# x loaded first, LayerNorm statistics ahead of the low matrices, and a prologue with one PSUM bank per block

## The chip, the cores and the metric

The kernel runs on one core of a Trainium2 chip. The metric is the device time of one execution in microseconds (us), the median of several. The engines are TensorE (PE in the profile, PEld its weight loads), VectorE (DVE), ScalarE (ACT), GpSimd (POOL) and SyncE (SP), which issues most of the transfers.

## The reference

A "macaron" block on x of 8 sequences, 512 tokens, 256 channels, all in float32:

```python
x = x + 0.5 * ffn(layernorm(x))
x = x + attn(layernorm(x))      # 16 heads, causal softmax, queries/keys/values of 2 x 256
x = x + 0.5 * ffn(layernorm(x)) # the same weights again

def ffn(x):
    h = x @ W_exp + b_exp                       # 256 -> 1024
    h = butterfly(h, up_weights, 1024)          # 10 stages of 2x2 mixing, stride 1, 2, ..., 512
    h = gelu(h + up_bias)                       # exact gelu
    h = butterfly(h, down_weights, 1024)        # 10 more stages
    return h @ W_con + b_con + down_bias        # 1024 -> 256
```

A butterfly is linear. The reference applies it to the activations.

## The kernel before

The kernel folds the butterflies into the weights first, in a prologue, and then works on the eight sequences with two plain matrices, `wup_sb` (256 to 1024) and `wdn_sb` (1024 to 256). The 1024 hidden features are 8 blocks (`NBLK`) of 128.

**The prologue.** The seven stages of small stride stay inside a block, so for each block they are one 128 x 128 matrix. `low_matrices` builds all eight on VectorE out of a table (`upe_sb`): six multiplications that double the width each time, from 32 to 1024 elements per partition (L225). `low_up` multiplies each with its rows of `wexp_sb` on PE (L254), 257 columns, the last one the bias. A float32 matmul is two passes in the profile. The three stages of large stride pair whole blocks. `high_stage` does one: per block ScalarE writes a product with the block's own coefficient (`mine`, L238), and VectorE adds the partner block times the other coefficient (L243). The result lies in `high_up`. `finish_up` transposes it on PE (`pup`, L269), four transposes to a PSUM bank, in the order first half of the blocks with both halves of the channels, then second half; ScalarE and VectorE copy the banks to `wup_sb` in turn. For the down side the same is done from `dne_sb` and `wcon_sb`, with `low_down` at the end (L275).

In between stands the first LayerNorm, of sequence 0: `ln_stats` (VectorE: two `bn_stats` and two `bn_aggr` per half and one addition, ten instructions in all; POOL: one power, `rstd`, per half), `ln_apply` on POOL (`xn`, L174, four instructions) and, in `ln_steps`, eight transposes on PE into two banks (`pxt`, L197), which ScalarE copies to `xnt` (L198). The first dense matmuls of the kernel, `ph_f` (L309), need both `xnt` and `wup_sb`. `keep_busy(19)` has PE multiply the identity with itself until `low_up` can run (`idle`, L261).

The order is written out by hand (`manual_schedule`): each engine executes its instructions in the order of the program text, here

```python
        keep_busy(19)
        mats = low_matrices(upe_sb, "up")
        cur = low_up(mats)
        run([partial(ln_stats, 0, "f1", half) for half in range(2)])
        run([partial(ln_apply, 0, "f1", half, nc.gpsimd) for half in range(2)])
        for i in range(HIGH):
            cur, whole = high_stage(cur, i, upc_sb, "up", C + 1, NBLK)
        run(ln_steps(0, "f1", copy=nc.scalar.copy))
        finish_up(cur, whole)
```

and waits are on semaphores between engines, per tile: two engines' accesses to one PSUM tile are put in order, reads too.

**PSUM.** It has eight banks. The kernel before has three pools from start to end: `ps_u` (one tile of four banks), `ps_o` (one bank) and `ps_a` (three single banks). `low_up` uses all of them: its first four blocks share the one tile of `ps_u`, the next three take the banks of `ps_a`, the last takes `ps_o`, which `idle` used before. `pxt` and `pup` then go round in the three banks of `ps_a`, so that each waits for the copy out of the tile three places earlier: the second `pup` bank takes the one that ScalarE's first copy to `xnt` has read.

**Transfers.** SP's queue issues, in this order: the two parts of `upe_sb` (0.5 MB each), the first half of `wexp_sb`, x of sequence 0, the second half of `wexp_sb`, then `dne_sb`, `wcon_sb` and the rest. ScalarE's queue brings the coefficients `upc_sb`.

**After the prologue** a table `ORDER` sets, for each sequence, how the steps of attention of one sequence and of the two feed-forward parts of its neighbours follow on one another.

Of the kernel before, what the change touches and what calls it, by code (L numbers as in the profile page):

```python
# [36 lines left out]
F32 = mybir.dt.float32  # L37
BF16 = mybir.dt.bfloat16
AF = mybir.ActivationFunctionType
# [3 lines left out]
P = 128  # L43
# [5 lines left out]
def macaron_kernel(  # L49
# [18 lines left out]
    nc = tc.nc  # L68
    B, N, C = x.shape
# [13 lines left out]
    lnp = ctx.enter_context(tc.tile_pool(name="ln", bufs=2))  # L83
    work = ctx.enter_context(tc.tile_pool(name="work", bufs=1))
    dram = ctx.enter_context(tc.tile_pool(name="dram", bufs=2, space=bass.MemoryType.DRAM))
    ps_u = ctx.enter_context(tc.tile_pool(name="ps_u", bufs=1, space=bass.MemoryType.PSUM))
    ps_o = ctx.enter_context(tc.tile_pool(name="ps_o", bufs=1, space=bass.MemoryType.PSUM))
    ps_a = ctx.enter_context(tc.tile_pool(name="ps_a", bufs=3, space=bass.MemoryType.PSUM))


    fold = ctx.enter_context(ExitStack())
    fold_pool = fold.enter_context(tc.tile_pool(name="fold", bufs=1))
    upc_sb = fold_pool.tile([P, HIGH, NBLK, 2], F32, name="upc_sb")
    dnc_sb = fold_pool.tile([P, HIGH, NBLK, 2], F32, name="dnc_sb")
    upb_sb = const.tile([P, NBLK], F32, name="upb_sb")
# [9 lines left out]
    def load_x(b):  # L105
        xt[b] = resid.tile([P, NT, C], F32, name=f"x_{b}", tag="x", bufs=4)
        nc.sync.dma_start(out=xt[b], in_=x[b].rearrange("(t p) c -> p t c", p=P))
# [10 lines left out]
    wexp_blocks = wexp_t.rearrange("(n p) c -> p n c", p=P)  # L118
    first, second = slice(0, NBLK // 2), slice(NBLK // 2, NBLK)
    with tc.manual_schedule():  # L120
        nc.sync.dma_start(out=upe_sb[:, :last], in_=up_e[:, :last])
        nc.sync.dma_start(out=upe_sb[:, last:], in_=up_e[:, last:])
        nc.sync.dma_start(out=wexp_sb[:, first, :], in_=wexp_blocks[:, first, :])
        load_x(0)
        nc.sync.dma_start(out=wexp_sb[:, second, :], in_=wexp_blocks[:, second, :])
        nc.scalar.dma_start(out=upc_sb, in_=up_c)
        nc.sync.dma_start(out=dne_sb, in_=dn_e)
        nc.sync.dma_start(out=wcon_sb, in_=wcon.rearrange("(n p) c -> p n c", p=P))
        nc.sync.dma_start(out=dnc_sb, in_=dn_c)
        nc.sync.dma_start(out=upb_sb, in_=up_b)  # L130
        nc.sync.dma_start(out=bc_sb, in_=b_con.to_broadcast([P, C]))
        nc.sync.dma_start(out=db_sb, in_=dn_b.to_broadcast([P, C]))
        load_x(1)
        for w_sb, w in ((wq_sb, wq), (wk_sb, wk), (wv_sb, wv), (wo_sb, wo)):
            nc.sync.dma_start(out=w_sb, in_=w.rearrange("(k p) f -> p k f", p=P))
        for b in range(2, 4):
            load_x(b)


    ident = const.tile([P, P], F32, name="ident")  # L140
    make_identity(nc, ident)

# [60 lines left out]
    def low_matrices(tables, net):  # L203

        at, mat = 0, None
        for step in range(LOW):  # L210
            half = 1 << step
            mine = tables[:, at : at + NBLK * 2 * half].rearrange("p (n e) -> p n e", n=NBLK)
            at += NBLK * 2 * half
            if mat is None:
                mat = mine
                continue
            new = fold_pool.tile([P, NBLK, 2 * half], F32, name=f"mat_{net}_{step}", tag=f"mat_{step % 2}")
            if net == "up":
                dims, old = "p n (a r) -> p n a r", mat.rearrange("p n (o r) -> p n o r", o=1)
                shape = dict(a=2)  # L220
            else:
                dims, old = "p n (m b) -> p n m b", mat.rearrange("p n (m o) -> p n m o", o=1)
                shape = dict(b=2)
            view = new.rearrange(dims, **shape)
            nc.vector.tensor_tensor(view, mine.rearrange(dims, **shape), old.to_broadcast(view.shape), ALU.mult)  # L225
            mat = new
        return mat

    def high_stage(cur, i, coef, net, width, on_scalar):

        tag = "wexp" if net == "dn" and i == 1 else f"high_{net}_{i % 2}"
        new = fold_pool.tile([P, NBLK, C + 1], F32, name=f"high_{net}_{i}", tag=tag)[:, :, :width]
        mine = []
        for blk in range(NBLK):
            mine.append(fold_pool.tile([P, width], F32, name=f"mine_{net}_{i}_{blk}", tag="mine", bufs=NBLK))
            w_self = coef[:, i, blk, 0:1]
            if blk < on_scalar:
                nc.scalar.activation(mine[blk], cur[blk], AF.Copy, scale=w_self)  # L238
            else:
                nc.gpsimd.tensor_scalar(mine[blk], cur[blk], w_self, 1.0, ALU.mult, ALU.mult)  # L240
        for blk in range(NBLK):
            w_other = coef[:, i, blk, 1:2]
            nc.vector.scalar_tensor_tensor(new[:, blk, :], cur[blk ^ (1 << i)], w_other, mine[blk], ALU.mult, ALU.add)  # L243
        return [new[:, blk, :] for blk in range(NBLK)], new

    def low_up(mats):

        four = ps_u.tile([P, 4, 512], F32, name="low_up", tag="u")
        banks = [four[:, i, :] for i in range(4)]
        banks += [ps_a.tile([P, 512], F32, name=f"low_up_{i}", tag="a") for i in range(3)]  # L250
        banks.append(ps_o.tile([P, 512], F32, name="low_up_o", tag="pa"))
        got = [bank[:, : C + 1] for bank in banks]
        for blk in range(NBLK):
            nc.tensor.matmul(got[blk], lhsT=mats[:, blk, :], rhs=wexp_sb[:, blk, :], start=True, stop=True)  # L254
        return got

    def keep_busy(times):

        idle = ps_o.tile([P, 512], F32, name="idle", tag="pa")
        for _ in range(times):  # L260
            nc.tensor.matmul(idle[:, :P], lhsT=ident, rhs=ident, start=True, stop=True)  # L261

# [16 lines left out]
    def ln_steps(b, what, **how):  # L279
        def new():  # L280
            kept["xnt", what, b] = work.tile([P, 4, KC, P], F32, name=f"xnt_{what}_{b}", tag="xnt", bufs=2)
            return kept["xnt", what, b]

        def step(kc):
            transposed(b, what, kept["xnt", what, b] if kc else new(), kc, **how)

        def write():
            td = kept["td", what, b] = dram.tile([P, 4, KC * P], F32, name=f"td_{what}_{b}", tag="td")
            nc.sync.dma_start(out=td, in_=kept.pop(("tx", what, b)).rearrange("p j k t r -> p j (k t r)"))

        def read():

            xnt = new().rearrange("p i k n -> p i (k n)")
            td = kept.pop(("td", what, b)).rearrange("(i s) j e -> j s i e", i=4)
            for j in range(4):
                nc.sync.dma_start(out=xnt[bass.ts(j, 32)], in_=td[j])

        if by_dma(b, what):
            return [write, read]
        return [partial(step, kc) for kc in range(KC)]  # L300
# [217 lines left out]
    def lns(b, what):  # L518

        return [partial(f, b, what, half) for f in (ln_stats, ln_apply) for half in range(2)]  # L520

    def run(*steps):
        for step in steps:
            if isinstance(step, list):
                run(*step)
            else:
                step()
# [99 lines left out]


    with fold, tc.manual_schedule():
        keep_busy(19)  # L630
        mats = low_matrices(upe_sb, "up")
        cur = low_up(mats)
        run([partial(ln_stats, 0, "f1", half) for half in range(2)])
        run([partial(ln_apply, 0, "f1", half, nc.gpsimd) for half in range(2)])
        for i in range(HIGH):
            cur, whole = high_stage(cur, i, upc_sb, "up", C + 1, NBLK)
        run(ln_steps(0, "f1", copy=nc.scalar.copy))
        finish_up(cur, whole)
        up = up_steps(0, "f1")
        mats = low_matrices(dne_sb, "dn")  # L640
        cur = [wcon_sb[:, blk, :] for blk in range(NBLK)]
        for i in range(HIGH - 1, -1, -1):
            cur, _ = high_stage(cur, i, dnc_sb, "dn", C, NBLK if i == HIGH - 1 else NBLK // 2)
            run([up.pop(0) for _ in range(min(3, len(up)))])
        nc.vector.tensor_tensor(bhalf, bc_sb, db_sb, ALU.add)
        nc.vector.tensor_scalar(bhalf, bhalf, 0.5, None, ALU.mult)
        low_down(mats, cur)
        run(partial(ffn_bias, 0, 0), partial(ffn_bias, 0, 1))
        run(lns(1, "f1"))

    with tc.tile_pool(name="attn", bufs=1) as attn, tc.manual_schedule():
        for b in range(B):
            sequence(b, attn)
# [77 lines left out]
```

## Time and profile before

| What | us |
|---|---|
| median of 3 runs | 886.3 |
| lowest and highest run | 885.77, 886.96 |
| the profiled execution | 884.92 |
| its span, first to last instruction | 883.1 |
| PE busy | 862.1 (98%) |
| VectorE busy | 628.0 (71%) |
| ScalarE busy | 520.1 (59%) |
| POOL busy | 87.1 (10%) |

Times in the profile count from the start of the span. The page cuts the span in 40 slices of 22 us and gives the busy share of each engine in tenths, and the clock that PE was granted, in tenths of full speed. The chain of waits is followed back from the last instruction to what released it, step by step. In rows of the timeline the first number is the start, the second the time that the row covers, "x8" the number of instructions in it, and the brackets say how long the engine was idle before, and what ended that. A row of a window that ends early can cover fewer instructions than the one of the whole stretch.

### The profile page before, as it was taken

What the parts mean: (1) busy time and instruction counts of PE and PEld (TensorE: products, weight loads), DVE (VectorE), ACT (ScalarE), POOL (GpSimd) and SP (SyncE); (2) the same over time, 40 slices, a digit from 0 to 9 for tenths busy, and PEclk for the clock granted to TensorE, in tenths of its full rate; (3) what the DMA queues carried; (4) which work ended last, traced back from release to release, by engine and by line L of the source; (5) the groups of instructions that cost most, each with busy time, mean ns of one, the idle gap of its engine ahead of it and who ended that gap; (6) DMA issues with size and microseconds to landing.
All of it is one profiled execution on the core that took longest, in us unless ns stands there. A gap on an engine that the chain in (4) does not pass through costs nothing.

```text
span 883.1 us, 13289 instructions
## 1 busy us (share of the span) xinstructions
PE 862.1 (98%) x4334; PEld 499.9 (57%) x4334; DVE 628.0 (71%) x1814; ACT 520.1 (59%) x1360; POOL 87.1 (10%) x103
## 2 busy tenths in 40 slices
PE   7999999999999999999999999999999999989988
PEld 5564644655546555555645646557555463745656
DVE  7957894998567775887758876877577775978230
ACT  5718676655495565875467663874458664746211
POOL 3420000021002010011102001021000000010010
PEclk8999999999999999999999999999999999999999
DMA  9210766548665667165774367666665477377600
GB/s 325 70 48 2 194 190 159 146 111 227 155 156 154 155 160 200 45 183 156 200 180 102 91 169 194 176 162 160 170 165 126 123 186 191 97 183 193 154 13 24
DMA packets 52964, 130.16 MB, mean 147 GB/s; under 512 B 10912, under 2 KB 32672, under 8 KB 52896
## 3 DMA queue, kind: packets, MB, share of 16 engines
q1 hardware_dynamic: 52752, 129.30, 55.5%
q8 instruction: 34, 0.56, 0.3%
q14 instruction: 34, 0.28, 0.1%
q10 hardware_dynamic: 144, 0.02, 0.0%
HBM read 21.80 MB, written 15.20 MB: 42 GB/s over the span
## 4 chain that ended last, share of the span: by engine, by line
PE 84%; DVE 8%; ACT 3%; DMA 2%; SPq 1%; issue 1%; POOL 0%; DVEq 0%; ACTq 0%; POOLq 0%
PE py_f L329 23%; PE ph_f L309 23%; PE pp L354 12%; PE sc L408 9%; PE pa L488 6%; PE pv L372 5%; PE po L509 5%; DVE e L422 4%; ACT e L435 2%; SPq L475 1%; DVE pr L453 1%; DVE high_up L243 1%; PE idle L261 1%; DMA td_f<-tx_f 1%; PE pup L269 0%
## 5 line engine op out<-in xcount | busy, mean ns | idle before, releaser
L435 ACT ACTIVATE e<-e,nm 128x128 f32<-128x128 f32 (+3 forms) x512 | 280.3, 549 | 112.7 <-DVE nm L422 112.4
L422 DVE CUSTOM_DVE_ANT_0 e<-sc,mask 128x128 f32<-128x128 f32 (+3 forms) x512 | 216.3, 485 | 117.2 <-PE sc L408 117.0
L329 PE MATMUL py_f<-wdn_sb,g_f 128*128 128x256 f32 x1024 | 232.7, 382 | 0.0
L309 PE MATMUL ph_f<-xnt_f,wup_sb 128*128 128x512 f32 x512 | 229.3, 596 | 1.1 <-ACT v L375 0.7
L329 PEld LDWEIGHTS py_f<-wdn_sb,g_f 128*128 128x128 f32 x1024 | 192.2, 190 | 43.8 <-issue 17.1
L453 DVE STREAM_TRANSPOSE pr<-e 128x1536 f32<-128x1536 f32 (+2 forms) x128 | 170.6, 1354 | 21.0 <-ACT e L435 20.9
L309 PEld LDWEIGHTS ph_f<-xnt_f,wup_sb 128*128 128x128 f32 x512 | 95.6, 190 | 113.3 <-issue 101.4
L316 ACT ACTIVATE g_f<-ph_f,bup_sb 128x512 f32<-128x512 f32 x128 | 85.2, 686 | 116.4 <-PE ph_f L309 116.0
L408 PE MATMUL sc<-kt,qt 32*128 32x128 f32 (+3 forms) x1024 | 92.2, 461 | 6.1 <-DVE nm L422 4.4
L435 ACT ACTIVATION_READ_ACCUMULATOR e<-e,nm 128x1 f32 x512 | 95.7, 187 | 0.0
L488 PE MATMUL pa<-pt,v 128*32 128x512 f32 (+3 forms) x1024 | 75.6, 435 | 1.8 <-issue 1.0
L408 PEld LDWEIGHTS sc<-kt,qt 32*128 32x128 f32 x1024 | 44.4, 183 | 57.2 <-issue 23.8
L160 POOL TENSOR_TENSOR rstd_f<-mv_f,mhalf 128x2 f32<-128x2 f32 x32 | 22.7, 710 | 483.4 <-DVE mv_f L158 483.3
L488 PEld LDWEIGHTS pa<-pt,v 128*32 128x32 f32 x1024 | 30.6, 109 | 57.8 <-issue 50.8
L354 PE MATMUL pp<-xnt_at,wq_sb 128*128 128x512 f32 x128 | 61.4, 602 | 0.0
L338 DVE SCALAR_TENSOR_TENSOR x<-py_f,x 128x512 f32<-128x512 f32 (+1 forms) x34 | 22.2, 652 | 55.2 <-PE py_f L329 55.2
L354 PE MATMUL pp<-xnt_at,wk_sb 128*128 128x512 f32 x128 | 60.9, 598 | 0.0
L509 PE MATMUL po<-wo_sb,ot 128*128 128x256 f32 x256 | 59.4, 384 | 0.0
L372 PE MATMUL pv<-wv_sb,xnt_at 128*128 128x512 f32 x128 | 59.1, 597 | 0.0
L435 ACT ACT_TABLE_LOAD x29 | 37.2, 1283 | 33.7 <-DVE nm L422 33.6
L509 PEld LDWEIGHTS po<-wo_sb,ot 128*128 128x128 f32 x256 | 47.6, 190 | 12.3 <-issue 4.7
L191 POOL TENSOR_TENSOR x<-x,bhalf 128x512 f32<-128x512 f32 x32 | 40.7, 1273 | 134.2 <-DVE xn_f L174 113.6
(74 smaller groups left out, 547.3 us busy)
## 6 DMA issues: line engine op xcount, KB each, us to landing
pt<-pr SPq DMA_DIRECT2D x512, 176.0 KB, 4.0
td_f<-tx_f SPq DMA_DIRECT2D x14, 512.0 KB, 5.0
xnt_f<-td_f SPq DMA_DIRECT2D x56, 128.0 KB, 3.0
x<-in_x_dram SPq DMA_DIRECT2D x8, 512.0 KB, 6.6
td_at<-tx_at SPq DMA_DIRECT2D x7, 512.0 KB, 2.6
xnt_at<-td_at SPq DMA_DIRECT2D x28, 128.0 KB, 3.1
out_dram<-x SPq DMA_DIRECT2D x14, 256.0 KB, 4.3
wexp_sb<-in_wexp_t_dram SPq DMA_DIRECT2D x2, 514.0 KB, 6.8
```

The source lines that it names most:

```text
L191: nc.gpsimd.tensor_tensor(x2, x2, bhalf.rearrange("p (o c) -> p o c", o=1).to_broadcast([P, 2, C]), ALU.add)
L309: nc.tensor.matmul(ph[:, :N], lhsT=wup_sb[:, kc, bass.ts(fc, P)], rhs=xnt[:, :, kc, :].rearrange("p i (t r) -> p t i r", r=32), start=(kc ...
L316: nc.scalar.activation(g[:, fc, :], ph[:, :N], AF.Gelu, bias=bup_sb[:, fc : fc + 1])
L329: nc.tensor.matmul(py[:, i, :], lhsT=g[:, fc, bass.ts(t, P)], rhs=wdn_sb[:, fc, :], start=(fc == 0), stop=(fc == NBLK - 1),)
L354: nc.tensor.matmul(pp[:, :N], lhsT=w[:, kc, bass.ts(g, P)], rhs=xnt[:, :, kc, :], start=(kc == 0), stop=(kc == KC - 1),)
L372: nc.tensor.matmul(pp, lhsT=xnt[:, t, kc, :], rhs=wv_sb[:, kc, :], start=(kc == 0), stop=(kc == KC - 1))
L408: nc.tensor.matmul(sc[:, j, at : at + n], lhsT=kept["q", b, gg][r, bass.ts(qb, P)], rhs=kept["k", b, gg][r, :n], start=(i == 0), stop=True ...
L422: nc.vector.tensor_tensor_reduce(out=e[:, j, at : at + n], in0=sc[:, j, at : at + n], in1=mask[:, N - n :], scale=-1.0, scalar=3.0e38, op0 ...
L435: nc.scalar.activation(e[:, j, at : at + n], e[:, j, at : at + n], AF.Exp, scale=-1.0, bias=nm[:, qb, gg, j : j + 1], accum_out=zs[:, gg, ...
L453: nc.vector.transpose(pr[:, :, :, qb : qb + 3 * n - 2 : 3, :].rearrange("p j h k r -> p h k j r"), blocks[:, :, :n])
L488: nc.tensor.matmul(by_row[r, :, kb * 32 :], lhsT=v[:, kb, bass.ds(g * P + j * HD, HD)], rhs=pt[:, :, bass.ds(j * NSLOT + SLOT[kb] + kb, NT ...
L509: nc.tensor.matmul(po[:, i, :], lhsT=ot[:, g, bass.ts(t, P)], rhs=wo_sb[:, g, :], start=(g == 0), stop=(g == NG - 1))
```

## The change

- x of sequence 0 is the first transfer on SP's queue; `upe_sb`'s two parts and the first half of `wexp_sb` come behind it. The second half of `wexp_sb` and all later transfers keep their places.
- `ln_stats` and `ln_apply` of sequence 0 stand ahead of `low_matrices`: VectorE does the ten statistics instructions first and then the six multiplications; POOL's `rstd` and `xn` follow the statistics as before.
- A tile `ones` of two elements is set by VectorE, and ScalarE's first instruction is a one-element activation on it, which takes the activation table load with it; before, the table load stood ahead of the first `mine`.
- `keep_busy` does 21 matmuls instead of 19.
- In the prologue PSUM is `ps_f`, five single banks, and `ps_a`, three single banks, as before. `low_up` gives each block a tile of one bank: five of `ps_f` (one of which `idle` had), three of `ps_a`. `ps_u` and `ps_o` are opened after the prologue, where `ps_f` was.

On every engine the instructions behind these keep their order.

```diff
-    ps_u = ctx.enter_context(tc.tile_pool(name="ps_u", bufs=1, space=bass.MemoryType.PSUM))
-    ps_o = ctx.enter_context(tc.tile_pool(name="ps_o", bufs=1, space=bass.MemoryType.PSUM))
     ps_a = ctx.enter_context(tc.tile_pool(name="ps_a", bufs=3, space=bass.MemoryType.PSUM))
 
     fold = ctx.enter_context(ExitStack())
     fold_pool = fold.enter_context(tc.tile_pool(name="fold", bufs=1))
+    ps_f = fold.enter_context(tc.tile_pool(name="ps_f", bufs=5, space=bass.MemoryType.PSUM))
...
     with tc.manual_schedule():
+        load_x(0)
         nc.sync.dma_start(out=upe_sb[:, :last], in_=up_e[:, :last])
         nc.sync.dma_start(out=upe_sb[:, last:], in_=up_e[:, last:])
         nc.sync.dma_start(out=wexp_sb[:, first, :], in_=wexp_blocks[:, first, :])
-        load_x(0)
         nc.sync.dma_start(out=wexp_sb[:, second, :], in_=wexp_blocks[:, second, :])
...
+    ones = fold_pool.tile([P, 2], F32, name="ones")
+    nc.vector.memset(ones, 1.0)
     ident = const.tile([P, P], F32, name="ident")
...
     def low_up(mats):
 
-        four = ps_u.tile([P, 4, 512], F32, name="low_up", tag="u")
-        banks = [four[:, i, :] for i in range(4)]
-        banks += [ps_a.tile([P, 512], F32, name=f"low_up_{i}", tag="a") for i in range(3)]
-        banks.append(ps_o.tile([P, 512], F32, name="low_up_o", tag="pa"))
-        got = [bank[:, : C + 1] for bank in banks]
+        got = []
         for blk in range(NBLK):
+            pool, tag = (ps_f, "f") if blk < 5 else (ps_a, "a")
+            got.append(pool.tile([P, 512], F32, name=f"low_up_{blk}", tag=tag)[:, : C + 1])
             nc.tensor.matmul(got[blk], lhsT=mats[:, blk, :], rhs=wexp_sb[:, blk, :], start=True, stop=True)
         return got
 
     def keep_busy(times):
 
-        idle = ps_o.tile([P, 512], F32, name="idle", tag="pa")
+        idle = ps_f.tile([P, 512], F32, name="idle", tag="f")
...
     with fold, tc.manual_schedule():
-        keep_busy(19)
+        nc.scalar.activation(ones[:, :1], ones[:, 1:2], AF.Copy)
+        keep_busy(21)
+        run([partial(ln_stats, 0, "f1", half) for half in range(2)])
+        run([partial(ln_apply, 0, "f1", half, nc.gpsimd) for half in range(2)])
         mats = low_matrices(upe_sb, "up")
         cur = low_up(mats)
-        run([partial(ln_stats, 0, "f1", half) for half in range(2)])
-        run([partial(ln_apply, 0, "f1", half, nc.gpsimd) for half in range(2)])
         for i in range(HIGH):
             cur, whole = high_stage(cur, i, upc_sb, "up", C + 1, NBLK)
...
+    ps_u = ctx.enter_context(tc.tile_pool(name="ps_u", bufs=1, space=bass.MemoryType.PSUM))
+    ps_o = ctx.enter_context(tc.tile_pool(name="ps_o", bufs=1, space=bass.MemoryType.PSUM))
     with tc.tile_pool(name="attn", bufs=1) as attn, tc.manual_schedule():
```

## The prediction

> **What bounds the kernel now.** I read the page first: which engine is busy, and in which slice it isn't.
>
> ```profile
> span 883.1 us, 13289 instructions
> ...
> PE   7999999999999999999999999999999999989988
> ...
> PEclk8999999999999999999999999999999999999999
> ```
>
> PE is busy all through except in the first slice (22 us), the only one with a lowered clock too. The change touches only that stretch, so the chain of waits (start, length) must show what sets the moment when dense matmuls begin there.
>
> ```profile
> 1.67 6.83 PE idle L261 x38
> 8.50 1.76 PE low_up L254 x8
> ...
> 10.28 1.58 ACT mine_up L238 x4
> ...
> 11.89 1.50 DVE high_up L243 x4
> ...
> 19.27 4.22 PE pup L269 x16
> 23.49 13.87 PE ph_f L309 x32
> ```
>
> From 23.3 us the chain is PE work without a gap until well past 60 us. So a shift of the first `ph_f` shifts the end. The timeline of that window shows VectorE's two waits for transfers, and ScalarE's copies that the sum will turn on:
>
> ```profile
> 4.65 0.19 DVE L225 TENSOR_TENSOR mat_up<-upe_sb 128x32 f32<-128x32 f32 x1 [4.65 <-DMA upe_sb<-in_up_e_dram]
> ...
> 8.98 0.43 DVE L156 BATCH_NORM_STATS2 st_f<-x 128x6 f32<-128x256 f32 x1 [1.10 <-DMA x<-in_x_dram]
> ...
> 19.56 1.07 ACT L198 COPY xnt_f<-pxt_f 128x512 f32<-128x512 f32 x2
> ```
>
> VectorE waits for `upe`, makes the low matrices until 7.88, waits for x until 8.98, and does the statistics until 11.63. These lie inside the time in which PE and ScalarE produce the first `low_up` and `mine_up`: only 0.26 us of VectorE idleness follows them. They were nearly hidden.
>
> **The change part by part.**
>
> *x first on SP's queue.* The first transfer was issued at 0.72 and released VectorE at 4.65. The next ones landed at issue plus time to landing: `upe`'s second part 5.96, `wexp`'s first half 7.4, x 8.98, `wexp`'s second half 10.46, thus 1.31 to 1.56 us each. x in front should land at 4.65 + (1.56 − 1.31) = 4.9 (bounds 4.65 and 5.2), the three transfers that it passes about 1.5 later (`upe` 6.2 and 7.5, `wexp` 9.0); from `wexp`'s second half on nothing moves.
>
> *Statistics ahead of the low matrices.* The ten instructions run from 8.98 to 11.63, 2.65 us: now 4.9 to 7.55. `upe` is there by then, so the statistics, not the transfer, hold the matrices. These take 4.65 to 7.88, 3.23 us: to 10.78 alone.
>
> *What the matrices now run beside.* POOL's two `rstd` (0.70 each) and four `xn` (1.22 each) start after the statistics, so `xn` runs from about 8.2, under the three long matrix multiplications. Before, nothing of POOL ran beside them. The nearest rows are these: VectorE's two-input operations, 0.40 us apart alone, start 0.62 apart beside POOL's `mine_dn` ((2.32 − 0.47) / 3, the last lasting 0.47), and the fourth `xn`, beside such operations, took 1.83 for 1.22.
>
> ```profile
> 30.58 2.32 DVE L243 SCALAR_TENSOR_TENSOR high_dn<-high_dn,dnc_sb,mine_dn 128x256 f32<-128x256 f32 x4
> ...
> 16.00 1.83 POOL L174 TENSOR_SCALAR xn_f<-x,mv_f,rstd_f 128x256 f32<-128x256 f32 x1
> ```
>
> Beside `xn` the `high_up` steps at 15.03 and 16.73 took 0.13 and 0.24 longer than the 0.395 pitch of their neighbours. Two `xn` fall under the matrices: 2 × 0.13 to 2 × 0.24; I take 0.35, with ends 0 and 0.75. Low matrices end at 11.13.
>
> The Trainium skill (SBUF — State Buffer, "Who interferes with whom") speaks against this change: a VectorE instruction with two SBUF inputs and a GpSimd instruction that reads SBUF exclude one another for the whole instruction. By that, three multiplications would each wait for a 1.22 us `xn`, 3.7 us instead of 0.35. The trace disagrees in size: `mine_dn` and `high_dn`, 0.47 and 0.40 us alone, alternate every 0.62, less than their sum.
>
> *PE.* `low_up` starts 0.07 after the matrices, L = 11.2 instead of 8.34 (+2.86). Two more idle matmuls (four passes) end by 9.6 even if the clock rises late; PE then has nothing for about 2 us. A 257-column pass takes 0.2175 (four between 8.77 and 9.64), so matmul k is done at L + 0.2175(2k + 1) + 0.38: 11.8 for the first, 14.84 for the last.
>
> *Single banks.* ScalarE started after four matmuls, 1.94 after L; now after the first, 0.62 after L. VectorE waited for four `mine`, now for two: first `high_up` at L + 1.03 + 0.49 + 0.08 = 12.8 (before 11.89). But PE's 0.435 per matmul now paces the stage: the last pair starts after `mine_7` at 15.4, and stage 1 at 16.2 instead of 15.03 (+1.2). Stages 1 and 2 take 6.95 less the 0.37 lost to `xn`, which is over by then: end 22.8 instead of 21.98 (+0.8).
>
> *ScalarE, the late one.* It issues its 16 `mine` of stages 1 and 2 at 0.40 from 0.38 after `mine_7` begins: 15.25 to 21.65, and only then the copies of `xnt`, 19.56 before. The second group of `pup` transposes takes the bank that the first copy frees: it began at 20.73 with the copy done at 20.15; now the copy ends at 21.65 + 0.59 = 22.24 and the group starts at 22.27 (+1.54), although VectorE's results would let it start by 21.5. From there the 12 transposes go as before, 0.213 each: first `ph_f` at 24.83 instead of 23.29. VectorE's copies, `dn` matrices and stages follow +1.5 too, so `low_dn` keeps its distance.
>
> *Costing nothing.* The early table load (1.28, no longer behind `upc`) and the one-element activation lie in ScalarE's wait until 10.28 (now 11.8); without that cover they would cost 1.28. The memset (0.1 to 0.2 by POOL's rows) lies in VectorE's wait for x. `xn` is ready by about 14, before PE is through with `low_up`. `ps_u` and `ps_o`, opened later, are first written near 68 us, when the last readers of their banks are done since 17. Later instructions keep their order on every engine.
>
> *Clock.* In windows of the profile (window, its length, PE busy, granted clock) it was granted fully until 16.8, 4.3 us after the last `low_up`, then half, and fully again from 23.6:
>
> ```profile
> 16.75:17.00 0.25, 0.00 (x0) 0.61 1.03 324
> ...
> 23.50:23.75 0.25, 0.25 (x1) 0.73 1.11 352
> ```
>
> That is 2.9 us after the dense `pup` began at 20.73; at the start 4.8 us passed, from 1.67 to about 6.5. In the new timeline PE does eight transposes and four scattered `pup` between 14.8 and 22.3, so it falls again, and rises 2.9 to 4.8 after 22.27: 0.35 to 2.25 us of `ph_f` at half speed, costing half of that, 0.17 to 1.13. Before it cost 0.17. I take +0.5, ends 0 and 1.0.
>
> The Trainium skill (TensorE: Matmul & The Clock Gate, Part 1) puts such changes on a free-running window of 3413 ns; 16.8 to 23.6 is two of them, which agrees. By it the rise may come 3.4 to 6.8 us after dense work begins, and my term would be an estimated 0.4 to 2.0, differing between executions.
>
> *Sum.* +1.54 + 0.5 = +2.0 us on the profiled execution's 884.92 (883.1 of span, 1.8 around it), 886.9. That execution is 1.4 below the median of the runs, 886.3, so I put the same sum on the median: 888.3. With x landing at its bounds (−0.25, +0.3), VectorE's contention (−0.35, +0.4) and the clock (−0.5, +0.5), the likeliest case spans +0.9 to +3.2: 887.2 to 889.5.
>
> **The rivals.**
>
> *Not slower: the clock stays up.* If transposes in the 7.4 us between `low_up` and the second `pup` group keep the clock, these 12 take 0.107 each instead of 0.213 (a quarter of the 0.43 that `ph_f`'s four times wider passes take, 13.87 / 32), −1.28, and `ph_f` loses nothing, −0.17: +1.54 − 1.45 = +0.1, 886.4. It decides if no stretch of about 4 us has so little PE work; against it, three scattered transposes did not hold it before 16.8.
>
> *The delay doesn't arrive.* If ScalarE's copies aren't late, VectorE's +0.8 alone counts: 887.1; with POOL leaving the matrices alone too, 886.8.
>
> *Port.* If POOL's 0.62 pitch there is not typical and three matrix multiplications each wait out an `xn` of 1.22 us, that is +3.7 for +0.35, thus +5.4, 891.7. For it: `xn` is 2.6 times as long as `mine_dn`. Against it: beside `xn`, VectorE lost 0.13 and 0.24.
>
> *Cold `low_up`.* If the idle 2 us drop the clock, eight matmuls take 0.87 each instead of 0.435: up to +3.5 more, 891.8. Against it: 4.3 us passed before it fell.
>
> **How the numbers follow.** A measurement tells about 0.2% (1.77 us) from no change. Forecast 0.66, three quarters of it above 888.07; the two mild rivals 0.16; port 0.09; cold `low_up` 0.05; an unseen gain 0.04. Slower 0.49 + 0.14 = 0.63, faster 0.04, the rest within. The range reaches into the mild rivals below and towards the costly ones above: 886.2 to 890.9.
>
> **What would show it.** Statistics from 4.9, matrices 7.6 to 11.1, `low_up` from 11.2, ScalarE's first `mine` after one matmul, second `pup` group released by ScalarE's copy at 22.2, `ph_f` near 24.8. I am wrong if x lands before 4 us, if `ph_f` starts before 24, or if PE gains gaps after 60 us.

## The result, and the profile after

| | before | after |
|---|---|---|
| median, us (6 runs each, side by side) | 887.01 | 890.24 |
| lowest and highest run | 885.77, 887.66 | 889.63, 893.12 |
| the profiled execution | 884.92 | 890.46 |
| its span | 883.1 | 888.7 |

The ratio of after to before is 1.0045, with a 95% interval of 1.0035 to 1.0055: slower by 4.0 us (3.1 to 4.9). It is estimated from all twelve runs; the two medians of the table differ by 3.2. The forecast was +2.0.

The page of the changed kernel, the same three rows as shown of before:

```profile
span 888.7 us, 13299 instructions
...
PE   6999999999999999999999999999999999989988
...
PEclk9899999999999999999999999999999999999999
```

The difference still lies at the start: the first slice of PE is less busy. But the clock row has moved: its lowered digit is now in the second slice (22 to 44 us), where the first `ph_f` run. A digit of 9 can still hide a loss, as the windows below show for the first slice.

The chain of waits of the changed kernel over the first 45 us (start, length, what):

```profile
5.00 0.44 DVE st_f L157
...
9.79 1.24 DVE mat_up L226
11.03 0.04 issue
11.07 5.00 PE low_up L253 x14
...
18.11 5.30 ACT mine_up L239 x13
23.40 0.48 ACT xnt_f L199
23.88 0.04 issue
23.92 2.82 PE pup L268 x12
26.74 15.06 PE ph_f L308 x32
41.80 3.21 PE low_dn L274 x14
```

Before, the chain went from idle matmuls through `low_up`, `mine`, `high_up` and `pup`. Now it comes from x's transfer, the statistics and the matrices, and ScalarE's copy to `xnt` releases the second `pup` group. That part is as forecast. Two lengths are not: `low_up` takes 5.00 for 14 passes, and the first 32 `ph_f` take 15.06 instead of 13.87.

The timeline of the changed kernel:

```profile
7.78 3.24 DVE L226 TENSOR_TENSOR mat_up<-upe_sb,mat_up 128x64 f32<-128x64 f32 x5
...
8.42 6.09 POOL L175 TENSOR_SCALAR xn_f<-x,mv_f,rstd_f 128x256 f32<-128x256 f32 x4
...
11.07 5.43 PE L253 MATMUL low_up<-wexp_sb,mat_up 128*128 128x257 f32 x16 [2.69 <-DVE mat_up L226]
...
23.92 2.82 PE L268 MATMUL pup<-ident,high_up 128*128 128x128 f32 x12 [0.52 <-ACT xnt_f L199]
...
26.54 15.26 PE L308 MATMUL ph_f<-xnt_f,wup_sb 128*128 128x512 f32 x32
```

PE stood idle for 2.69 us, waiting for the matrices, and then needed 5.43 us for 16 passes that take 3.64 at full clock (in the first experiment below).

In the kernel before, the same `ph_f` in the timeline and `low_dn` in the chain:

```profile
23.29 14.08 PE L309 MATMUL ph_f<-xnt_f,wup_sb 128*128 128x512 f32 x32
```

```profile
37.36 3.65 PE low_dn L275 x16
```

The profile's +5.6 us of span adds up like this. The first `ph_f` starts at 26.54 instead of 23.29 (+3.25), of which `low_up` at half clock is 1.8. The first 32 `ph_f` take 1.19 longer. From `low_dn` on, at 41.80 instead of 37.36, the distance stays near 4.4 until about 850 us. At the end the transposes ahead of the last `ph_f` take 0.2 longer and these `ph_f` 14.93 instead of 14.00, because the clock fell there in this execution. The +4.0 of the runs is below this one execution's +5.5, so such parts differ between executions.

The granted clock says why. In 0.25 us steps it leaves 1.00 at 12.21, is back at 15.63, falls at 22.46 and is back at 29.28 (the moments worked out from the share of the step in which it changes). These are 3.42, 6.83 and 6.82 apart: multiples of one period of 3.41. So here are windows of the changed kernel cut at these moments (window, length, PE busy, PEld, VectorE, ScalarE, POOL, granted clock, DMA share, GB/s):

```profile
8.80:12.21 3.41, 1.14 (x5) 1.03 (x6) 2.15 (x2) 0.40 (x1) 3.41 (x3) 1.00 1.06 409
12.21:15.63 3.42, 3.42 (x9) 2.71 (x9) 1.75 (x4) 2.03 (x6) 2.30 (x2) 0.50 1.07 373
15.63:19.04 3.41, 2.16 (x12) 1.23 (x11) 2.87 (x8) 3.33 (x9) 0.00 (x0) 1.00 1.06 332
19.04:22.46 3.42, 0.65 (x2) 0.28 (x2) 3.31 (x10) 3.42 (x9) 0.00 (x0) 1.00 1.06 382
22.46:25.87 3.41, 2.83 (x12) 2.32 (x12) 2.69 (x7) 2.37 (x6) 0.21 (x1) 0.50 1.03 330
25.87:29.28 3.41, 3.41 (x9) 1.86 (x8) 2.36 (x6) 3.35 (x9) 0.00 (x0) 0.50 0.24 78
```

Read each row with the clock of the row under it. A window with PE busy for 1.14 of 3.41 us is followed by half clock, although its last 1.1 us were dense `low_up`. A full window brings the clock back. 2.16 of 3.41 keeps it, 0.65 loses it, 2.83 doesn't bring it back, 3.41 does. The trace of before, cut in the same way at its own changes, follows the same reading:

```profile
9.98:13.40 3.42, 2.27 (x10) 1.44 (x8) 3.02 (x11) 3.12 (x9) 2.39 (x3) 1.00 1.00 394
13.40:16.81 3.41, 0.96 (x3) 0.42 (x3) 3.41 (x10) 3.41 (x10) 3.41 (x4) 1.00 0.99 295
16.81:20.23 3.42, 2.28 (x8) 1.46 (x8) 3.32 (x9) 3.42 (x10) 1.01 (x1) 0.50 1.05 370
20.23:23.64 3.41, 3.41 (x15) 3.16 (x16) 2.47 (x7) 1.95 (x5) 0.20 (x1) 0.50 1.07 368
```

So before, too, the clock was lost, but in a stretch in which PE had only transposes, and it came back 0.35 us after the first `ph_f`. The Trainium skill (TensorE: Matmul & The Clock Gate, Part 1) describes a free-running window of 3413 ns; these rows agree in the period, and add from which share of a window the clock was lost and won here.

The mean granted clock of single executions is on record too. One window of 3.41 us at half clock lowers it by 0.002 (1.7 of 883 us), and in all twelve profiles of this document it agrees with the windows counted in them: 0.996 for the two of before, 0.992 for the four of the changed kernel (the one at 12.21, the two from 22.46 on, and one at the end). Half clock ahead of the first listed change isn't in it. Four of the six executions of the changed kernel have 0.992.

The theory after this: the change costs the delay of the matrices (about +1.5 us at `ph_f`) plus the clock that PE's idle 2.7 us lose (`low_up` at half speed, then `ph_f`). Rivals: the cost is the order itself, with a cold PE as a side effect; the cost comes from the single banks; it comes from x's place in the queue.

### The profile page after: what moved, and what is told of

Read it like the earlier page. It is cut to its first block, busy times and chain, and to the rows that moved or that the text cites. A ratio compares the mean times of both kernels' runs of the same rounds, so it can differ in the third digit from the quotient of the medians.

```text
span 888.7 us, 13299 instructions
## 1 busy us (share of the span) xinstructions
PE 865.4 (97%) x4338; PEld 501.9 (56%) x4338; DVE 627.8 (71%) x1815; ACT 520.9 (59%) x1361; POOL 87.5 (10%) x103
## 4 chain that ended last, share of the span: by engine, by line
PE 82%; DVE 9%; ACT 4%; DMA 3%; SPq 1%; issue 1%; DVEq 0%; POOL 0%; ACTq 0%; POOLq 0%
PE ph_f L308 23%; PE py_f L328 22%; PE pp L353 12%; PE sc L407 9%; PE pa L487 6%; PE pv L371 5%; PE po L508 4%; DVE e L421 4%; ACT e L434 2%; SPq L474 1%; DVE pr L452 1%; DMA td_f<-tx_f 1%; ACT mine_up L239 1%; DVE xn_f L175 1%; PE low_up L253 1%
```

## The experiments

Each ratio is to runs of the kernel before on the same chip at the same time. Kernels measured at different times are compared by these ratios; 0.001 is 0.89 us.

**Filling the gap.** The changed kernel with 13 more idle matmuls, so that PE works until `low_up` can start:

```diff
-        keep_busy(21)
+        keep_busy(34)
```

> The changed kernel with 34 idle matmuls instead of 21, so that PE works until the low matrices are there (about 11.1 us). Theory (the statistics delay the low matrices, and in the uncovered 2.7 us PE's clock falls): low_up runs at full speed, 3.6 instead of 5.4 us for its 16 passes, the first ph_f begins near 24.8 instead of 26.5, and the time is 1.5 to 2.5 us below the changed kernel's, near 888. Rival (the delay alone, or the banks, cost the time; the clock adds nothing): no change within 0.5 us.

Measured: 888.79 us (7 runs; before 887.06), ratio 1.0026 (1.0015 to 1.0038). The timeline, and below it lines of the chain:

```profile
11.38 3.64 PE L253 MATMUL low_up<-wexp_sb,mat_up 128*128 128x257 f32 x16
```

```profile
25.27 14.36 PE ph_f L308 x32
39.64 3.64 PE low_dn L274 x16
```

`low_up` starts 0.31 later than in the changed kernel, ends 1.5 earlier, and `low_dn` comes 2.16 earlier (39.64 for 41.80). In time it is 1.7 us by the ratios, although the intervals (1.0035 to 1.0055, and 1.0015 to 1.0038) overlap a little. Nothing but idle work was added, so the clock is a cause of its own, worth nearly half of the loss by these ratios. The clock then falls later, at 19.58, after a window with PE busy 0.60 of 3.41.

**The order alone.** The kernel before with x first and the statistics ahead of the matrices; its PSUM pools, its 19 idle matmuls and the table load stay:

```diff
+        load_x(0)
         nc.sync.dma_start(out=upe_sb[:, :last], in_=up_e[:, :last])
...
-        load_x(0)
...
-        mats = low_matrices(upe_sb, "up")
-        cur = low_up(mats)
         run([partial(ln_stats, 0, "f1", half) for half in range(2)])
         run([partial(ln_apply, 0, "f1", half, nc.gpsimd) for half in range(2)])
+        mats = low_matrices(upe_sb, "up")
+        cur = low_up(mats)
```

> The kernel before with x loaded first and the statistics ahead of the low matrices, and nothing else of the change (19 idle matmuls, the tile of four banks, the late table load). Theory (the order costs, the single banks win back a part): low matrices end near 11.0, ScalarE starts only after four matmuls (about 13.5 to 15), first ph_f at 27 to 28.5, the time 0.5 to 2.5 us above the changed kernel's. Rival (the single banks cost time): below the changed kernel's time, near 888.

Measured: 889.88 us (5 runs; before 887.06), ratio 1.0036 (1.0023 to 1.0050): about the whole loss, and not told apart from the changed kernel's. The timeline:

```profile
11.09 4.99 PE L254 MATMUL low_up<-wexp_sb,mat_up 128*128 128x257 f32 x14 [3.38 <-DVE mat_up L225]
...
14.32 2.67 ACT L238 ACTIVATE mine_up<-low_up,upc_sb 128x257 f32<-128x257 f32 x7 [8.69 <-PE low_up L254]
```

ScalarE waits for four blocks, until 14.32. The first `ph_f` comes at 26.98, 0.44 later than in the changed kernel, where the single banks let it start earlier. In time these banks win nothing that could be measured here.

**The banks alone.** The kernel before with `ps_f`'s single banks and nothing else of the change:

```diff
-    ps_u = ctx.enter_context(tc.tile_pool(name="ps_u", bufs=1, space=bass.MemoryType.PSUM))
-    ps_o = ctx.enter_context(tc.tile_pool(name="ps_o", bufs=1, space=bass.MemoryType.PSUM))
...
+    ps_f = fold.enter_context(tc.tile_pool(name="ps_f", bufs=5, space=bass.MemoryType.PSUM))
...
+            pool, tag = (ps_f, "f") if blk < 5 else (ps_a, "a")
+            got.append(pool.tile([P, 512], F32, name=f"low_up_{blk}", tag=tag)[:, : C + 1])
```

> The kernel before with the prologue's PSUM in single banks and nothing else of the change. Theory: ScalarE starts after the first low_up, near 9.0 instead of 10.3, but VectorE is held by the statistics until 11.6, so the first high_up starts 0.2 us earlier and later steps up to 0.8 earlier: 0 to 1 us below the kernel before. Rival (the banks cost): 1 to 3 us above it.

Measured: 886.70 us (10 runs; before 887.06), ratio 0.9997 (0.9987 to 1.0006): no difference. The timeline:

```profile
8.85 1.78 ACT L237 ACTIVATE mine_up<-low_up,upc_sb 128x257 f32<-128x257 f32 x4 [2.49 <-PE low_up L251]
...
11.74 3.23 DVE L242 SCALAR_TENSOR_TENSOR high_up<-low_up,upc_sb,mine_up 128x257 f32<-128x257 f32 x8
```

ScalarE begins 1.43 earlier than before (10.28), but the first `high_up` only 0.15 earlier (11.89), since VectorE is held by the statistics, whose last instruction starts at 11.64 in this trace. So the banks are not the cost, and the gain was behind VectorE.

**Two gaps filled.** The changed kernel with 34 idle matmuls, and 12 more between `pxt` and `pup`, where the clock fell next:

```diff
-        keep_busy(21)
+        keep_busy(34)
...
         run(ln_steps(0, "f1", copy=nc.scalar.copy))
+        keep_busy(12)
         finish_up(cur, whole)
```

> The changed kernel with 34 idle matmuls at the start and 12 more between the transposes of xn and those of high_up, where PE waits 3.5 us. Theory (part of the loss is half clock in the pup transposes and the first ph_f): pup's 12 dense transposes take 0.11 instead of 0.21 each and no ph_f pass is slow: 1.5 to 2.5 us below the variant with 34 idle matmuls alone, 886 to 887. Rival (the clock adds nothing there): equal to that variant within 0.5 us, or above it where the fillers delay pup.

Measured: 887.72 us (10 runs; before 887.06), ratio 1.0012 (1.0003 to 1.0022), 1.2 below the one gap filled by the ratios, where 1.5 to 2.5 were expected. The wait in the timeline, and the window that ends where the clock fell:

```profile
22.30 2.49 PE L268 MATMUL pup<-ident,high_up 128*128 128x128 f32 x12 [0.66 <-ACT xnt_f L199]
```

```profile
19.31:22.72 3.41, 1.74 (x8) 0.97 (x8) 3.31 (x9) 3.41 (x10) 0.00 (x0) 1.00 1.06 379
```

The 12 last only until 19.3; the wait for `high_up` (0.82 us) and the wait for ScalarE's copy (0.66) leave PE 1.74 of 3.41 busy, and the clock still falls at 22.72, in the middle of `pup`. So the clock was kept for longer, but not through. What is left is +1.1 us (0.3 to 2.0). It isn't the pure delay: in the profiles the first `ph_f` comes 1.3 later than before's (24.59) and `low_dn` 1.88 (39.24), but nine of this kernel's ten executions had only one window at half clock (mean clock 0.998), while 19 of the 23 of the kernel before had three (0.994), the third probably at the end of the kernel, where the experiment on it below finds such falls.

**The clock alone, without the change.** The kernel before with 6 idle matmuls instead of 19; its order is untouched:

```diff
-        keep_busy(19)
+        keep_busy(6)
```

> The kernel before with 6 idle matmuls at the start instead of 19, nothing else: PE idles from about 4.3 us to low_up at 8. Theory (PE's clock at low_up, not only the time at which the matrices are there, sets the prologue): low_up runs at half clock, its 16 passes last 5.5 to 7 us instead of 3.7, first ph_f 1.0 to 3.0 us later, the time 0.8 to 3 us above the kernel before, in which not one instruction was reordered. Rival (the order of the statistics is all): within 0.4 us of the kernel before.

Measured: 888.08 us (10 runs; before 886.24), ratio 1.0024 (1.0013 to 1.0035), slower by 2.1 us. The timeline, and two windows of `low_up` (length, PE busy, granted clock, DMA share, GB/s):

```profile
8.08 5.61 PE L254 MATMUL low_up<-wexp_sb,mat_up 128*128 128x257 f32 x14 [3.48 <-DVE mat_up L225]
```

```profile
9.00:10.00 1.00, 1.00 (x4) 1.00 1.24 427
...
13.00:14.00 1.00, 1.00 (x6) 1.00 1.08 385
```

Nothing in the order, the transfers or the banks differs from before, and `low_up` even starts 0.26 earlier. A cold `low_up`, with what follows from it, loses 2.1 us; `low_dn` comes 2.05 later than before in this profile (39.41 for 37.36). The clock column is of no use here: it says 1.00 in both windows, while four passes touch the first microsecond and six the second, and 14 take 5.61 where 16 take 3.64 at full clock. It shows no lowered value ahead of the first change that it lists.

**x first, with the old order on VectorE.** The changed kernel with the statistics put back behind the matrices:

```diff
-        run([partial(ln_stats, 0, "f1", half) for half in range(2)])
-        run([partial(ln_apply, 0, "f1", half, nc.gpsimd) for half in range(2)])
         mats = low_matrices(upe_sb, "up")
         cur = low_up(mats)
+        run([partial(ln_stats, 0, "f1", half) for half in range(2)])
+        run([partial(ln_apply, 0, "f1", half, nc.gpsimd) for half in range(2)])
```

> The changed kernel with the statistics back behind the low matrices on VectorE; x stays the first transfer. Theory (the order on VectorE is most of the delay, the transfer order the smaller part): upe lands near 6.2, low matrices end near 9.5 instead of 11.0, statistics end near 12.2; PE's uncovered gap shrinks to about 1 us and the clock stays; first ph_f at 24 to 24.8, time 887 to 888.5. Rival (x ahead of upe is the cost, the order costs nothing): low matrices end near 11, time as the changed kernel's.

Measured: 887.55 us (10 runs; before 886.73), ratio 1.0006 (0.9997 to 1.0016). The timeline:

```profile
6.34 0.19 DVE L226 TENSOR_TENSOR mat_up<-upe_sb 128x32 f32<-128x32 f32 x1 [5.49 <-DMA upe_sb<-in_up_e_dram]
...
6.57 2.99 DVE L226 TENSOR_TENSOR mat_up<-upe_sb,mat_up 128x64 f32<-128x64 f32 x5
...
9.66 3.72 PE L253 MATMUL low_up<-wexp_sb,mat_up 128*128 128x257 f32 x16 [0.76 <-DVE mat_up L226]
```

The matrices wait for `upe`, which x delays by 1.69, and `low_up` starts 1.3 later than before. But PE's gap is only 0.76 and the clock stays. At the first `ph_f` 0.55 is left of it (23.84). So x's place in the queue, with the banks, costs 0.5 us by the ratio, not told from none, and at most 1.4 by its interval; the order on VectorE carries the loss. The five matrices take 2.99 here, with POOL quiet, and 3.24 in the changed kernel beside `xn`: running beside POOL costs 0.25.

**Half of the statistics ahead.** The changed kernel with half 0 of `ln_stats` ahead of the matrices, half 1 and POOL's part behind `low_up`:

```diff
-        run([partial(ln_stats, 0, "f1", half) for half in range(2)])
-        run([partial(ln_apply, 0, "f1", half, nc.gpsimd) for half in range(2)])
+        ln_stats(0, "f1", 0)
         mats = low_matrices(upe_sb, "up")
         cur = low_up(mats)
+        ln_stats(0, "f1", 1)
+        run([partial(ln_apply, 0, "f1", half, nc.gpsimd) for half in range(2)])
```

> The changed kernel with only the first half's statistics ahead of the low matrices, the second half's behind them. Theory (VectorE's wait between x and upe, 5.0 to about 6.3 us, has room for 1.3 us, half of the 2.65 that the change puts there): the half is free, low matrices run 6.4 to 9.6, PE's uncovered gap is about 1 us and the clock stays, second half done near 10.9, first high_up near 11.3, low_dn in the profile at 37 to 38.5, time 886 to 887.5. Rival (any statistics ahead delay the matrices by their length): low matrices end near 10.9, time 888.5 to 890.

Measured: 887.38 us (10 runs; before 886.24), ratio 1.0013 (0.9999 to 1.0027), with runs from 884.91 to 889.90, a spread of 5 us where the other kernels with ten runs spread by 1.2 to 3.8. The profiled execution is one of the slowest (889.62). Its timeline, and the window that ends with the loss of the clock:

```profile
10.15 5.42 PE L253 MATMUL low_up<-wexp_sb,mat_up 128*128 128x257 f32 x16 [2.15 <-DVE mat_up L226]
```

```profile
7.96:11.37 3.41, 1.26 (x7) 1.08 (x7) 3.24 (x8) 0.48 (x2) 0.00 (x0) 1.00 1.09 400
```

x landed at 5.60 here, later than in the changed kernel (5.00), and the gap before `low_up` was 2.15 us: inside one window, and enough. So `low_dn` came at 40.94, not at the 37 to 38.5 expected, although the median is as expected. A gap of this size can fall into one window or be split by two, and an execution's luck with that would explain the spread. The times do go with the clock: the three executions of 884.91 to 885.57 us have a mean granted clock of 0.996, two windows at half clock, and those from 887.17 us on have 0.994 to 0.990, three to five. But none of the three was profiled, so that they differ by the gap ahead of `low_up` is argued, not shown.

**The bank that waits for ScalarE.** The kernel with two gaps filled, and in it `pup` takes its banks from `ps_f`, so that it doesn't wait for the copies to `xnt`:

```diff
-                pt = ps_a.tile([P, 512], F32, name=f"pup_{kc}_{q}", tag="a")
+                pt = ps_f.tile([P, 512], F32, name=f"pup_{kc}_{q}", tag="f")
```

> The variant with 34 and 12 idle matmuls, and the pup transposes in ps_f's banks, so that they no longer wait for the bank that ScalarE's copies to xnt free. Theory (that wait holds the second pup group by about 0.6 us): the group starts when the first ends, near 21.7 instead of 22.3, the first ph_f 0.3 to 0.6 us earlier, the time 0.3 to 0.6 below that variant's. Rival (VectorE's results hold the group anyway): no change within 0.2 us.

Measured: 888.14 us (10 runs; before 886.73), ratio 1.0024 (1.0015 to 1.0033). The timeline:

```profile
20.52 3.54 PE L268 MATMUL pup<-ident,high_up 128*128 128x128 f32 x16 [0.82 <-DVE high_up L244]
...
29.49 0.70 PE L308 MATMUL ph_f<-xnt_f,wup_sb 128*128 128x512 f32 x1 [0.28 <-ACT g_f L315]
```

The wait is gone: all 16 `pup` run in one stretch of 3.54 at a clock granted fully, and the first `ph_f` comes at 23.89, 0.7 ahead of the kernel with two gaps filled, although the 34 idle matmuls overran and `low_up` began 0.4 later (11.63). This shows that the bank was the gate. But the time did not fall; it is even 1.1 above by the ratios, with intervals that overlap. 0.28 is lost to a new wait for ScalarE's gelu, and the profiled execution's last `ph_f` took 15.55 instead of 14.00. None of the ten executions was without half clock: seven have a mean of 0.998, one window, which the profiled one has at its end, while the kernel with two gaps filled has its one window in the prologue. Where it lies in the executions that were not profiled isn't known, so this miss stays open.

**The end of the kernel.** The kernel before with seven idle matmuls ahead of the last sequence's transposes, where PE waits for the last LayerNorm (`k7` is a new step in the order table):

```diff
-              ... 2a2+0 2x2+0 8g+0
+              ... 2a2+0 k7 2x2+0 8g+0
```

> The kernel before with 7 extra idle matmuls (1.5 us) at its end, in the 4.4 us between the last py of sequence 6 and the last sequence's ph_f, where PE has only eight transposes. Theory (part of the spread of all these kernels, and 1.1 of the changed profile's 5.5 us, is the clock falling there in some executions, whatever the prologue does): the last sequence's ph_f takes 14.0 us in its profile and the median falls by 0.3 to 1.2 us below the kernel before. Rival (the end has no part in it): the same within 0.3 us, or up to 0.5 above.

Measured: 885.76 us (10 runs; before 886.73), ratio 0.9995 (0.9986 to 1.0004): the sign is as expected, the size isn't told from none. By the mean granted clock seven of these ten executions had two windows at half clock (0.996), of the kernel before ten of 31, and the others three (0.994). The last `ph_f` took 14.00 us in both kernels that were given this filler; of ten profiled executions without it, four show 14.00 and six 14.93 to 16.24. So the end can lose 0.9 to 2.2 us in an execution.

**A version put together from these.** The changed kernel with x behind `upe_sb`'s two parts and ahead of `wexp_sb`, the statistics behind the matrices again, `pup` in `ps_f`, 16 idle matmuls between `low_up` and `pxt`, and `k7` at the end; the single banks, the 21 idle matmuls and the early table load stay:

```diff
-        load_x(0)
         nc.sync.dma_start(out=upe_sb[:, :last], in_=up_e[:, :last])
         nc.sync.dma_start(out=upe_sb[:, last:], in_=up_e[:, last:])
+        load_x(0)
...
+        mats = low_matrices(upe_sb, "up")
+        cur = low_up(mats)
         run([partial(ln_stats, 0, "f1", half) for half in range(2)])
         run([partial(ln_apply, 0, "f1", half, nc.gpsimd) for half in range(2)])
-        mats = low_matrices(upe_sb, "up")
-        cur = low_up(mats)
...
+        keep_busy(16)
         run(ln_steps(0, "f1", copy=nc.scalar.copy))
```

> A version meant to beat both: single banks and the early table load from the change; upe first, then x, then wexp; low matrices first, then the statistics; 21 idle matmuls at the start, 16 between low_up and the transposes of xn, 7 at the end; pup in ps_f's banks. Theory: low_up from about 9.0, statistics done near 10.8, first high_up at 10.9 (before 11.9), high_up ends near 20.8 (before 22.0), pup and ph_f at full clock, first ph_f at 21.3 to 22.3, time 883.5 to 885.5. Rival (x ahead of wexp delays low_up as much as it saves): as the kernel before, 887.

Measured: 883.79 us (10 runs; before 886.73), ratio 0.9973 (0.9964 to 0.9983): 2.4 us faster than before. The page and the timeline:

```profile
PEclk9999999999999999999999999999999999999999
```

```profile
9.32 3.72 PE L253 MATMUL low_up<-wexp_sb,mat_up 128*128 128x257 f32 x16 [0.90 <-DVE mv_f L158]
12.88 3.73 PE L260 MATMUL idle<-ident 128*128 128x128 f32 x32
16.45 1.35 PE L198 MATMUL pxt_f<-ident,xn_f 128*128 128x128 f32 x8
18.42 3.54 PE L268 MATMUL pup<-ident,high_up 128*128 128x128 f32 x16 [0.62 <-DVE high_up L244]
21.79 5.32 PE L308 MATMUL ph_f<-xnt_f,wup_sb 128*128 128x512 f32 x12
```

PE's gaps are 0.90 and 0.62 us, the clock never falls in this execution (the mean is 1.000 in seven of ten), and the first `ph_f` starts at 21.79, 1.5 earlier than in the kernel before, although `low_up` starts 1.0 later (9.32 for 8.34). What each part of this version is worth was not measured by itself.

## Why the prediction was wrong in its size

**x first: right.** It landed at 5.00 (4.9 forecast).

**Statistics ahead of the matrices: right.** 5.00 to 7.65 (4.9 to 7.55); the matrices ended at 11.03 (11.13), `low_up` started at 11.07 (11.2). What POOL's work beside them cost was 0.25 us (3.24 against 2.99), inside the ends of 0 and 0.75 and below the 0.35 taken. The rival with the port fell: no multiplication waited out an `xn`.

**ScalarE as the late one: right.** The second `pup` group waited for the copy of `xnt`, in the trace as forecast, and the kernel in which `pup` has its own banks had no such wait. That gate came at 23.92 instead of 22.27, because what stood ahead of it ran slower.

**"Costing nothing": not contradicted.** No such piece is in the chain of the changed kernel.

**The clock: the step that failed.** The prediction costed `low_up` at full clock, and dismissed the rival of a cold one with "4.3 us passed before it fell". That 4.3 us was a distance from the last dense work to the fall in one trace, and it was read as a time that PE may be idle. Cut into windows at the changes themselves, the same trace had already shown another thing: the fall came after one window of 3.41 us with PE busy for 0.96, however long the gap, and the distance depends on where the window lies. In the changed kernel the window from 8.80 to 12.21 had PE busy for 1.14, and the clock fell. The term taken was +0.5, for `ph_f` alone. It measured 1.8 (`low_up` 5.43 for 3.64) plus 1.19 (`ph_f`) in the profiled execution, 3.0 in all. The part for `ph_f` was too small because the clock rose at 29.28, 5.4 us after the dense `pup` began at 23.92, where the sum took 2.9 to 4.8; the 3.4 to 6.8 that the prediction worked out from the window held. With the forecast delay of 1.54 that makes 4.5, against the 4.44 in the trace behind `ph_f`; in the trace the delay is 1.45 (3.25 less 1.8).

The times of the runs agree with that split, within intervals of about 1 us each way. Filling the gap took off 1.7 us by the ratios, filling the second one another 1.2, together 2.9 of the 4.0; what remained is +1.1 where the forecast had 1.54 for the delay, but that rest holds the end of the kernel too, and doesn't confirm the 1.54. A cold `low_up`, with no step moved, cost 2.1.

The falls of the clock at the end of the kernel were in no term either. The sum started from a profiled execution of before with a mean clock of 0.996, two windows at half clock, while on two of the three chips most other executions of that kernel have three (0.994). The measured 890.24 lies inside the stated 886.2 to 890.9, but only because that range reached towards the costly rivals, and not by the sum.

So the case to which 0.05 was given, a cold `low_up`, is what happened. Its price, "up to +3.5 more" for all eight matmuls at half speed, was too high in turn: the half clock began at 12.21, in the fifth of 16 passes, and ended at 15.63, in the 13th. The two milder rivals fell with the same rows: the clock did not stay up, and the delay did arrive.

## What to carry to other kernels

Before work is put ahead of what PE waits for, draw PE's new timeline and cut it in windows of the period that the granted clock's changes show, at several phases: a gap costs its own length once, and the work behind it a second time if the window is mostly empty. Read the share of a window, not the length of a gap. When the order has to stay, filling the gap with idle matmuls is a cheap test of how much of the loss is clock, and if single banks or an earlier transfer are to gain, the engine that consumes them must be free by then.

## What the runs showed of the hardware

- Cut at the clock's own changes, the prologues of before, after and eight of the other kernels read alike. A fall followed a window of 3.41 us with PE busy for 0.60 to 1.74 us (18% to 51%). Windows at full clock that kept it had 1.63 (48%) and more, so the border lies near one half, no sharper than that. At half clock, windows with 1.04 to 2.89 us (30% to 85%) did not bring it back, and every return followed a full one.
- Transposes on PE by themselves brought the clock back: before's window from 20.23 to 23.64 held nothing but `pup`, except in its last 0.35 us.
- The granted clock is listed as 1.00 ahead of the first change that is listed, even where passes run at half speed (the kernel before with 6 idle matmuls).
- Where the windows lie differs between executions: the fall in the middle of the prologue came at 16.81 us in the kernel before, and at 17.50 in the one that differs from it only at the end of the kernel. There `low_dn` started at 37.36 and at 37.94 (`low_up` at 8.34 and 8.66).
